# Layer 0 and self-attention of 32 images: another first image, another running minimum, another last convolution

## The chip, the cores and the metric

The kernel runs on one core of a Trainium2 chip. Its time is the device time of one execution in microseconds. The core has five engines with a queue each: TensorE (PE in the profile; PEld are its weight loads), VectorE (DVE), ScalarE (ACT), GpSimd (POOL) and SyncE (SP, which here only issues DMAs). They run independently and wait for one another through semaphores. Matmuls write into PSUM[...]; all else lives in SBUF.

## The reference

The input x has shape (32, 64, 56, 56): 32 images of 64 channels and N = 3136 pixels. All is float32.

```python
# layer 0: within each of 8 groups of 8 channels, all products of two and of three channels
x = x + (conv2(products of 2) + b2) * beta2 + 0.1 * (conv3(products of 3) + b3) * beta3
# layer 1, for each image, l is the result of layer 0
g = clip(batchnorm(w_inside @ l), 0, 6)        # (64, N)
theta = l[:32]                                 # (32, N)
f = theta.T @ theta                            # (N, N)
f = softmax(softmax(f, axis=1), axis=2)        # once over the rows, once over the columns
out = g @ f.T / 56 * 56
out = batchnorm(depthwise_conv3x3(out)) + l
```

f is symmetric, so a softmax over its first axis and one over its second can be made from the same rows of scores.

## The kernel before

**Pairs and tiles.** Images are worked on in 16 pairs A and B. The N rows of an image's scores are cut into tiles of 128; the tiles of a pair are 24 of A, one for the tails of both, and 24 of B: IT = 49, and 784 in all. `scores` (L477 on) makes a tile in two halves of 1568 columns: four matmuls theta^T theta of 392 columns into the four banks of a PSUM tile `ps` (of which there is one), then one eviction on DVE, `e<-ps`. It copies the half into an SBUF tile `e` (of which there are four), times 1.0, and its accumulator writes the maximum of each row into `mx`. After both halves `first_softmax` reduces the two maxima on DVE to `nm`, the negated maximum, and ACT makes Exp(e + nm) with the sum of each row; for the tile before, `second_softmax` takes the reciprocal of that sum on DVE and ACT makes the second Exp. LAG = 3 tiles later `attend` multiplies the tile with g on PE into `av` and `ax` (banks of PSUM). A pair's result is divided on DVE, turned and brought by DMA into `tt`.

**Layer 0.** `products` multiplies channels with shifted channels: for a chunk of columns (PCS: 13 chunks of 242, the last 232) and two groups of 32 slots. `load_next` loads x with the channels shifted over the partitions (tiles `x`, `xa`, `xb`), and the centre channels (`xc`), which takes two DMAs whose source is two groups of 32 rows. The products are multiplied with the weights on PE (`poly`), and `poly_out` adds a bias and the centre channels on DVE and writes `y`, the layer's result. For all images but the first the products are made on POOL, and matmuls and outputs are spread over the tiles of the pair before; the second image's work lies in the tiles of the first. For the first image there is nothing to spread it over: its products are made on DVE, its loads are issued by SP and ACT by turns, and `first_poly` writes its sums into PSUM banks of their own (`pp`, `pq`). The row groups of g are made behind the chunks (`first_g`). Then `load_theta` copies theta from `y` to the four partition groups by four DMAs, and the first tile's scores can begin.

**The convolution.** The depthwise convolution of pair n is 45 steps on DVE: NB = 5 blocks of rows times 9 taps, each a SCALAR_TENSOR_TENSOR (`y` = `tt` shifted times a weight, plus `y`); `conv_begin` adds the bias on POOL first, `store` writes a finished block to `out`. The steps are spread over the gaps of the next pair's tiles. The last pair has no next pair: its 45 steps follow its last tile back to back.

**What sets the order.** Every engine's order is written out: `Pinned` makes each instruction follow the one issued before it on the same engine, and its helper `call` is line L109, the line of every instruction in the profile. The loop over tiles issues work by slots ("loads", "feed", "gap0", "gap1", "aux0") that `put` fills by tile number; `feed` and `advance` issue loads and products as their buffers come free and as a budget (`credit`) allows. At most eight DMAs are under way at a time: they go through eight semaphores in turn.

Of the kernel before, what the change touches and what calls it, by code (L numbers as in the profile page):

```python
# [9 lines left out]
FP = mybir.dt.float32  # L10
AF = mybir.ActivationFunctionType
ALU = mybir.AluOpType
AX = mybir.AxisListType
# [20 lines left out]
NK = 3  # L34
# [36 lines left out]
def tile_poly_conv_attention(  # L71
# [123 lines left out]

    b3row = const.tile([128, C], FP, name="b3row")
# [13 lines left out]
    dve.tensor_tensor(bias0, bias0, t0, ALU.add)  # L210

# [9 lines left out]
    for k in range(GM):  # L221
# [13 lines left out]
    yt = yp.tile([128, 3, N], FP, name="y")  # L235
    ys = [yt[:, p, :] for p in range(3)]
    pool.memset(ys[0][C:, :], 0.0)
    prods = {}
    NB = 5
    BLK = [(b * H // NB, (b + 1) * H // NB) for b in range(NB)]  # L240
    stored = set()

    LOADS = {
        "0": [(0, 1, 0, 0)],
        "a": [(0, 1, 0, 1)],
        "2": [(0, 1, 2, 0)],
        "4": [(0, 1, 4, 0)],
        "b": [(0, 2, 5, 0), (1, 2, 1, 0)],  # L250
    }
# [11 lines left out]
    def start(out, in_, queue=sync):  # L263
        credit[0] -= 1
        queue.dma_start(out=out, in_=in_)

    def load_next():
        tag, key = plan.pop(0)
        n, c, ks, name, k, queue = key
        p0, w = PCS[c]  # L270
        held[tag] += 1
        ident = f"{n}_{c}_{ks[0]}_{k}"
        if name == "c":
            t = xp.tile([128, 2, PCH], FP, name=f"xc_{ident}", tag=tag, bufs=XB[tag])
            at = slice(ks[0] * 32, ks[-1] * 32 + 32)
            for d in range(2):
                src = bass.AP(
                    x.tensor,
                    ((4 * n + ks[0]) * EXT + 4 * d) * 4 * N + p0,
                    [[EXT * 4 * N, len(ks)], [N, 32], [1, w]],  # L280
                )
                start(t[at, d, :w], src, queue)
            loaded[key[:-1]] = [t[at, d, :w] for d in range(2)]
            return
        t = xp.tile([128, PCH], FP, name=f"x{name}_{ident}", tag=tag, bufs=XB[tag])
        for s0, every, d, grow in LOADS[name]:
            src = bass.AP(
                x.tensor,
                ((4 * n + k) * EXT + d) * 4 * N + p0,
                [[N, 32], [grow * 4 * N, NSLOT // every], [1, w]],  # L290
            )
            start(t[s0::every, :w] if every > 1 else t[:, :w], src, queue)
        loaded[key[:-1]] = t[:, :w]
# [9 lines left out]
    def products(n, c, ks, eng):  # L303
# [16 lines left out]
        for k in ks:  # L320
            yield "load", (n, c, ks, "a", k)
            x0[k] = use("0", k)
            xa = use("a", k)
            q = prp.tile([128, PCH], FP, name=f"q_{ident}_{k}", tag="q", bufs=ROOM["q"])[:, :w]
            eng.tensor_tensor(q, x0[k], xa, ALU.mult)
            rounds[0][k] = q
            held["xs"] -= 1
            prefetch()
        for r, of in enumerate(("0", "2", "4", "b")):
            rounds.append({})  # L330
            yield "pr", len(ks)
            for k in ks:
# [4 lines left out]
                eng.tensor_tensor(p, rounds[0][k], xr, ALU.mult)  # L337
# [8 lines left out]
        eng.tensor_tensor(p4, both[0], both[1], ALU.mult)  # L346
# [27 lines left out]
    def feed(n, c, ks, eng):  # L374
# [3 lines left out]
        for tag, name, k in todo:  # L378

            queue = act if eng is dve and len(plan) % 2 else sync  # L380
            plan.append((tag, (n, c, ks, name, k, queue)))
        feeds.append((products(n, c, ks, eng), None))
# [12 lines left out]
    def poly(n, c, ks, rs, acc=None):  # L395

# [3 lines left out]
        own = acc is not None  # L402
        if not own:
            acc = ax[:, AUX:]
        at = slice(ks[0] * 32, ks[-1] * 32 + 32)
        for r in rs:
            for k in ks:
                pe.matmul(
                    out=acc[k * 32 : k * 32 + 32, :w],
                    lhsT=wq[:, r, k % 2, :] if r < NRND else w4[at, k * 32 : k * 32 + 32],  # L410
                    rhs=rounds[r][k],
                    start=own and r == 0,
# [5 lines left out]
    def poly_out(n, c, ks, acc=None):  # L418

        if acc is None:  # L420
            acc = ax[:, AUX:]
# [6 lines left out]
            ys[n % 3][at, p0 : p0 + w], acc[at, :w], bias0[at], xc, ALU.add, ALU.add  # L428
# [5 lines left out]
    def load_theta(b):  # L434
        y = ys[b // 2 % 3]
        p0 = (b % 2) * C
        th = thp.tile([128, N], FP, name=f"th_{b}", tag=f"th{b % 2}")
        for r in range(4):
            start(th[r * 32 : r * 32 + 32, :], y[p0 : p0 + CRED, :])
        ths[b] = th  # L440
# [36 lines left out]
    def scores(t, half):  # L477
        n, kind, q = tile_at(t)
        if half == 0:
            es[t] = ep.tile([128, N], FP, name=f"e_{t}", tag="e")  # L480
            mx = sp.tile([128, 2], FP, name=f"mx_{t}", tag="mx")
            nm = sp.tile([128, 1], FP, name=f"nm_{t}", tag="nm")
            z = sp.tile([128, 1], FP, name=f"z_{t}", tag="z")
            rz = sp.tile([128, 1], FP, name=f"rz_{t}", tag="rz")
            stats[t] = mx, nm, z, rz
        p = ps.tile([128, HALF, BANK], FP, name=f"ps_{t}_{half}", tag="ps")
        for j in range(HALF):
# [12 lines left out]
        e = es[t][:, half * HALF * CH : (half + 1) * HALF * CH]  # L500
        dve.tensor_scalar(
            e.rearrange("p (j c) -> p j c", c=CH), p[:, :, :CH], 1.0, None, ALU.mult, ALU.max,
            accum_out=stats[t][0][:, half : half + 1],
        )

    def first_softmax(t):
        mx, nm, z, _ = stats[t]
        dve.tensor_reduce(nm, mx, AX.X, ALU.max, negate=True)
        act.activation(es[t], es[t], AF.Exp, bias=nm, scale=1.0, accum_out=z)

    def second_softmax(t):
        _, _, z, rz = stats.pop(t)
# [82 lines left out]
    def conv_begin(n, b):  # L595
        blk = ys[n % 3][:, BLK[b][0] * W : BLK[b][1] * W]
        pool.tensor_scalar(blk, blk, bias2, None, ALU.add)

    def conv_step(n, i):
        b, i = divmod(i, 9)  # L600
        k, dy, dx = TAPS[i]
        r0, r1 = max(BLK[b][0], 1 - dy), min(BLK[b][1], H + 1 - dy)
        x0, x1 = max(0, 1 - dx), min(W, W + 1 - dx)
# [10 lines left out]

    def store(n, b):
        stored.add((n, b))
        blk = slice(BLK[b][0] * W, BLK[b][1] * W)
# [73 lines left out]
    put(-1, "aux0", lambda: [feed(0, c, ONE, dve) for c in range(NPC)])  # L691
    put(-1, "aux0", lambda: prepare(FOR_G))
    banks = {}

    def bank(c):
        k, r = divmod(c, HALF + NK)
        if r == 0:
            t = ps.tile([128, HALF, BANK], FP, name=f"pp_{k}", tag="ps")
            banks.update({k * (HALF + NK) + i: t[:, i, :] for i in range(HALF)})
        if r >= HALF:  # L700
            banks[c] = pa.tile([128, BANK], FP, name=f"pq_{c}", tag=f"av{r - HALF}")
        return banks[c]

    def first_poly(c):
        acc = bank(c)
        for r in range(NRND + 1):
            advance()
            poly(0, c, ONE, [r], acc)
        advance()
        poly_out(0, c, ONE, acc)  # L710

    def first_g(c):
        for qs in GS:
            if ready(qs) == c:
# [4 lines left out]
    for c in range(NPC):  # L719
        put(-1, "aux0", lambda c=c: first_poly(c))  # L720
        if c:
            put(-1, "aux0", lambda c=c: first_g(c - 1))
    put(-1, "aux0", lambda: load_theta(0))
    put(-1, "aux0", lambda: first_g(NPC - 1))

# [5 lines left out]
    for n in range(NP):  # L731
# [50 lines left out]
        if n == 0:  # L782
            put(0, "feed", lambda: [feed(0, c, TWO, pool) for c in range(NPC)])
        if n + 1 < NP:
            put(
                max(base - 8, 1), "feed",
                lambda n=n: [feed(n + 1, c, ALL, pool) for c in range(NPC)],
# [10 lines left out]
    for n in range(NP):  # L798
        t0 = n * IT + IT + LAG + 5
        more = range(2 * t0, 2 * ((n + 2) * IT - 1))  # L800
        if n + 1 < NP:
            more = [h for h in more if h // 2 != (n + 1) * IT + NQ + LAG]
            more = [h for h in more if h not in leaves] if len(more) - len(leaves & set(more)) >= 9 * NB else more
        for i in range(9 * NB):
            at = more[i * (len(more) - 1) // (9 * NB - 1)] if n + 1 < NP else 2 * t0 + i
# [10 lines left out]
    run(-1, "aux0")  # L816
# [119 lines left out]
```

## Time and profile before

| what | value |
| --- | --- |
| time, median of 3 runs | 5033.5 us (5032.83 to 5038.3) |
| the profiled execution's own time | 5033.6 us |
| its span in the profile | 5031.8 us |
| granted TensorE clock, mean over the span | 0.983 |
| first eviction starts at | 146.92 us |
| one pair in the middle (first eviction to the next pair's first) | 295.15 us |
| the first pair | 404 us |
| the last pair's convolution starts at | 4988.90 us |

The span is the time from the first recorded instruction to the last. A row of the timeline reads: start, duration in us, engine, line, operation, output<-inputs by tile name, shapes, and how many instructions are merged in it; in brackets the idle time of the engine just before and what ended it. A row of the groups has the busy sum and the mean of one in ns, then the idle time before and its releaser. A row of the stretches gives busy time (and number of instructions) of each engine between two times, then the granted TensorE clock as a share of full speed, the mean busy share of the 16 DMA engines and the bandwidth. A float32 matmul appears as two records.

### The profile page before, as it was taken

Reading aid. Unit: us, or ns where it says so; the run is one execution under the profiler, and the core shown is the slowest. Engines: PE = TensorE matmul, PEld = TensorE weight load, DVE = VectorE, ACT = ScalarE, POOL = GpSimd, SP = SyncE. Lnnn points to the kernel's source line nnn. Section 1 sums busy time; section 2 is a strip of 40 time slices with the busy share of each in tenths; the row PEclk is TensorE's granted clock in tenths of the full one; section 3 lists DMA queues with packets and bytes.
Section 4 is the critical chain, followed back from the end, with each engine's and each line's share of the span. In section 5 each row is a group of like instructions: output and inputs, shape, how many; then the busy total and the mean of one; then the engine's idle time right before and its main releaser. Section 6 shows DMA issues by size and latency. Waiting matters only on the chain.

```text
span 5031.8 us, 240733 instructions
## 1 busy us (share of the span) xinstructions
PE 4753.8 (94%) x105924; PEld 3340.6 (66%) x105924; DVE 4222.6 (84%) x6962; ACT 4545.5 (90%) x2356; POOL 3194.2 (63%) x4325
## 2 busy tenths in 40 slices
PE   3898999999999999999999999999999999999995
PEld 1465676776767677676766767676676767667663
DVE  4465698898989889898988989898898989889887
ACT  0577899999999999999999999999999999999995
POOL 0667585876858587585857758586775858677000
PEclk7899999999999999999999999999999999999998
DMA  5555656555565555655565565556556555654201
GB/s 144 140 153 152 150 147 149 145 146 143 143 147 144 147 142 144 145 147 139 152 149 137 142 148 148 139 149 149 143 137 145 151 142 145 151 139 120 44 10 33
DMA packets 892956, 684.17 MB, mean 136 GB/s; under 512 B 291584, under 2 KB 877568, under 8 KB 887808
## 3 DMA queue, kind: packets, MB, share of 16 engines
q1 hardware_dynamic: 879368, 659.52, 51.4%
q8 instruction: 828, 13.57, 1.1%
q10 hardware_dynamic: 12536, 9.25, 0.7%
q14 instruction: 224, 1.84, 0.1%
HBM read 565.65 MB, written 25.69 MB: 118 GB/s over the span
## 4 chain that ended last, share of the span: by engine, by line
PE 71%; DVE 21%; DMA 4%; issue 2%; POOL 1%; SPq 1%; ACT 0%; ACTq 0%; POOLq 0%; DVEq 0%
PE av L109 30%; PE ps L109 24%; PE ax L109 16%; DVE e L109 15%; DVE y L109 3%; DMA xc_None<-in_x_dram 2%; DVE num L109 1%; DMA xa<-in_x_dram 1%; SPq L109 1%; POOL p L109 1%; DMA x<-in_x_dram 1%; DVE rd L109 0%; DVE nm L109 0%; POOL q L109 0%; DMA xb<-in_x_dram 0%
## 5 line engine op out<-in xcount | busy, mean ns | idle before, releaser
L109 DVE TENSOR_SCALAR_CACHE_REDUCE e<-ps 128x1568 f32<-128x1568 f32 x1568 | 2806.6, 1790 | 508.1 <-PE ps L109 462.9
L109 PEld LDWEIGHTS av<-gq,e 128*64 128x64 f32 x64512 | 2014.1, 138 | 864.7 <-issue 806.7
L109 ACT ACTIVATE e<-e,nm 128x3136 f32<-128x3136 f32 x784 | 2282.8, 2912 | 310.8 <-DVE rz L109 228.3
L109 POOL TENSOR_TENSOR p<-q,x 128x242 f32<-128x242 f32 (+1 forms) x2418 | 1781.1, 769 | 939.6 <-PE ax L109 843.0
L109 ACT ACTIVATE e<-e,rz 128x3136 f32<-128x3136 f32 x784 | 2270.3, 2896 | 0.0
L109 PE MATMUL av<-gq,e 128*64 128x65 f32 x64512 | 2227.2, 225 | 3.9 <-ACT e L109 3.2
L109 PE MATMUL ps<-th 32*128 32x392 f32 (+1 forms) x12800 | 1489.4, 541 | 109.7 <-DVE e L109 96.7
L109 PEld LDWEIGHTS ps<-th 32*128 32x128 f32 (+1 forms) x12800 | 491.3, 181 | 448.0 <-DVE e L109 368.4
L109 DVE SCALAR_TENSOR_TENSOR y<-tt,wdt,y 128x605 f32<-128x605 f32 (+4 forms) x720 | 742.4, 1032 | 6.7 <-DMA tt<-tr 5.3
L109 POOL TENSOR_TENSOR p<-q,xb 128x242 f32<-128x242 f32 x806 | 592.5, 762 | 230.6 <-PE ax L109 218.1
L109 POOL TENSOR_TENSOR q<-x,xa 128x242 f32<-128x242 f32 x806 | 561.5, 722 | 216.0 <-DMA xa<-in_x_dram 208.2
L109 PE MATMUL ax<-gq,e 128*64 128x65 f32 x12288 | 489.7, 222 | 0.0
L109 PE MATMUL ax<-p,wq 128*32 128x242 f32 (+1 forms) x6448 | 481.5, 373 | 1.5
L109 PEld LDWEIGHTS ax<-gq,e 128*64 128x64 f32 x12288 | 425.3, 138 | 0.0
L109 POOL TENSOR_SCALAR y<-y,bias 128x616 f32<-128x616 f32 (+1 forms) x80 | 162.8, 2036 | 147.5 <-PE ax L109 137.7
L109 PEld LDWEIGHTS ax<-p,wq 128*32 128x32 f32 x6448 | 178.9, 109 | 111.4 <-POOL p L109 18.8
L109 DVE SCALAR_TENSOR_TENSOR y<-ax,bias,xc_None 128x242 f32<-128x242 f32 (+3 forms) x208 | 97.1, 467 | 108.8 <-PE ax L109 103.1
L109 POOL TENSOR_TENSOR p<-xc_None 128x242 f32<-128x242 f32 (+3 forms) x208 | 127.6, 614 | 78.8 <-DMA xc_None<-in_x_dram 68.6
L109 PE MATMUL ax<-wit,y 128*64 128x64 f32 x3136 | 143.8, 223 | 18.6 <-DVE ax L109 9.6
L109 PE MATMUL ax<-p,w 128*32 128x242 f32 (+1 forms) x1612 | 123.9, 369 | 31.6 <-POOL p L109 31.6
L109 ACT ACTIVATION_READ_ACCUMULATOR e<-e,nm 128x1 f32 x784 | 145.6, 186 | 0.0
L109 DVE TENSOR_REDUCE nm<-mx 128x1 f32<-128x2 f32 x784 | 121.7, 155 | 27.2
(73 smaller groups left out, 1368.1 us busy)
## 6 DMA issues: line engine op xcount, KB each, us to landing
x<-in_x_dram SPq DMA_DIRECT2D x2268, 121.0 KB
xb<-in_x_dram SPq DMA_DIRECT2D x1512, 60.5 KB
xa<-in_x_dram SPq DMA_DIRECT2D x756, 121.0 KB
th<-y SPq DMA_DIRECT2D x128, 392.0 KB
xc_None<-in_x_dram SPq DMA_DIRECT2D x360, 121.0 KB
x<-in_x_dram SPq DMA_DIRECT2D x190, 116.0 KB
out_dram<-y SPq DMA_DIRECT2D x64, 308.0 KB
tt<-tr SPq DMA_DIRECT2D x128, 100.0 KB
```

The costliest lines, as they stand in the source:

```text
L109: i = f(*args, **kw)
```

## The change

1. **The first image** is worked in 7 chunks of 448 columns (FCS), by functions of its own. `first_loads` issues 16 DMAs per chunk, by SP and ACT in turn, into a ring of 28 slots in the four `e` tiles; the centre channels are loaded in four DMAs of 32 rows. `first_products` makes 11 products on DVE into 21 slots that lie in `y`'s two later parts and in `tt`. `first_poly`, `first_out` and `first_g` follow one chunk apart. Theta is copied in two parts, the first five chunks and the rest, and the second image's first twelve loads are issued between the two.
2. **The running minimum.** The eviction multiplies by −1 and accumulates the minimum; the second half starts from the first half's minimum, read from `nm`. The TENSOR_REDUCE is gone; the first Exp takes scale −1 and the minimum as its bias.
3. **The last pair's convolution** has 7 blocks of 8 rows. Blocks 0 to 3 are steps on DVE as before; blocks 4 to 6 are 27 matmuls of `tt` with diagonal matrices of the tap weights (`make_diags`, on POOL early in the last pair) into one PSUM tile, and a DVE operation per block merges them with the bias and `y`.

The diff, cut to its core (the parameters `queue` and `eng` of `feed`, `products` and `start` and the accumulator parameter of `poly` fall away, since only POOL's products are left there):

```diff
+    FW = N // 7
+    FCS = [(p, FW) for p in range(0, N, FW)]
+    firsts = [ep.tile([128, N], FP, name=f"first_{i}", tag="e") for i in range(4)]
...
+    fx, fp = parts(firsts), parts(ys[1:] + [tt])
...
+    def first_loads(c):
+        p0, w = FCS[c]
+
+        def load(dst, k, d, grow, steps):
+            src = bass.AP(x.tensor, (k * EXT + d) * 4 * N + p0, [[N, 32], [grow * 4 * N, steps], [1, w]])
+            if steps == 1:
+                src = bass.AP(x.tensor, (k * EXT + d) * 4 * N + p0, [[N, 32], [1, w]])
+            (act if fat["q"] % 2 else sync).dma_start(out=dst, in_=src)
+            fat["q"] += 1
+
+        for name, k in [(a, k) for k in (0, 1) for a in "0a"] + [(a, k) for a in "24b" for k in (0, 1)]:
...
+            for s0, every, d, grow in LOADS[name]:
+                load(t[s0::every, :] if every > 1 else t, k, d, grow, NSLOT // every)
+        for d in (0, 1):
...
+            for k in (0, 1):
+                load(t[k * 32 : k * 32 + 32, :], k, 4 * d, 0, 1)
+
+    def first_products(c):
...
+        q = {k: product(xs["0", k], xs["a", k]) for k in (0, 1)}
+        frs[c] = [q] + [{k: product(q[k], xs[a, k]) for k in (0, 1)} for a in "024b"]
+        dve.tensor_tensor(xs["c", 1], xs["c", 0], xs["c", 1], ALU.mult)
+
+    first_loads(0)
+    first_loads(1)
+    first_products(0)
...
+    first_products(1)
+    first_loads(2)
...
-    BLK = [(b * H // NB, (b + 1) * H // NB) for b in range(NB)]
+    BLK = [[(b * H // NB, (b + 1) * H // NB) for b in range(NB)]] * (NP - 1)
+    BLK.append([(r, r + 8) for r in range(0, H, 8)])
+    NDVE = 4
...
-    def load_theta(b):
+    def load_theta(b, c0=0, c1=N):
...
-            start(th[r * 32 : r * 32 + 32, :], y[p0 : p0 + CRED, :])
+            start(ths[b][r * 32 : r * 32 + 32, c0:c1], y[p0 : p0 + CRED, c0:c1])
...
         dve.tensor_scalar(
             e.rearrange("p (j c) -> p j c", c=CH),
-            p[:, :, :CH], 1.0, None, ALU.mult, ALU.max,
-            accum_out=stats[t][0][:, half : half + 1],
+            p[:, :, :CH], -1.0, nm[:, :1] if half else None, ALU.mult, ALU.min,
+            accum_out=nm[:, half : half + 1],
         )
...
     def first_softmax(t):
-        mx, nm, z, _ = stats[t]
-        dve.tensor_reduce(nm, mx, AX.X, ALU.max, negate=True)
-        act.activation(es[t], es[t], AF.Exp, bias=nm, scale=1.0, accum_out=z)
+        nm, z, _ = stats[t]
+        act.activation(es[t], es[t], AF.Exp, bias=nm[:, 1:], scale=-1.0, accum_out=z)
...
+    def make_diags():
+        eye = xp.tile([128, PCH], FP, name="eye", tag="xs", bufs=XB["xs"])[:, :128]
+        pool.memset(eye, 0.0)
+        pool.affine_select(out=eye, in_=eye, ...)
+        for k in range(9):
...
+            pool.tensor_scalar(t, eye, wdt[:, k : k + 1], None, ALU.mult)
+
+    def conv_matmuls(n, blocks):
+        acc = ps.tile([128, HALF, BANK], FP, name="conv", tag="ps")
+        for j, b in enumerate(blocks):
+            for i in range(9):
...
+                pe.matmul(
+                    out=o[:, r0 - rb : r1 - rb, x0:x1],
+                    lhsT=diags[k],
+                    rhs=tr[:, r0 + dy - 1 : r1 + dy - 1, x0 + dx - 1 : x1 + dx - 1],
...
+    def conv_end(n):
+        blocks = range(NDVE, len(BLK[n]))
+        accs = conv_matmuls(n, blocks)
+        done = 0
+        for b in range(NDVE):
+            for i in range(9):
+                conv_step(n, 9 * b + i)
+            store(n, b)
+            while done < len(blocks) and (b + 1) * len(blocks) >= (done + 1) * NDVE:
+                m = blocks[done]
+                y = ys[n % 3][:, BLK[n][m][0] * W : BLK[n][m][1] * W]
+                dve.scalar_tensor_tensor(y, accs[m], bias2, y, ALU.add, ALU.add)
+                store(n, m)
+                done += 1
...
+    fb = ps.tile([128, HALF, BANK], FP, name="first_s", tag="ps")
+    banks = [fb[:, i, :] for i in range(HALF)]
+    banks += [pa.tile([128, BANK], FP, name=f"first_{i}", tag=f"av{i}") for i in range(NK)]
...
+    first_poly(0)
+    for c in range(1, NF):
+        first_poly(c)
+        first_out(c - 1)
+        if c + 2 < NF:
+            first_loads(c + 2)
+        if c + 1 < NF:
+            first_products(c + 1)
+        if c == 5:
+            load_theta(0, 0, FCS[5][0])
+            for b in range(NPC):
+                feed(0, b, TWO)
+            credit[0] = 12
+            advance()
+        first_g(c - 1)
+    first_out(NF - 1)
+    load_theta(0, FCS[5][0], N)
+    first_g(NF - 1)
...
+        if n + 1 == NP:
+            put(n * IT + LAG + 1, "feed", make_diags)
...
+            put(t0, "gap0", lambda n=n: conv_end(n))
```

## The prediction

> **What bounds the kernel now.** I read the engine totals first, then the chain that ended last, then busy time by stretch.
>
> ```profile
> span 5031.8 us, 240733 instructions
> PE 4753.8 (94%) x105924; PEld 3340.6 (66%) x105924; DVE 4222.6 (84%) x6962; ACT 4545.5 (90%) x2356; POOL 3194.2 (63%) x4325
> ...
> core 0: us, PE busy (x) PEld busy (x) DVE busy (x) ACT busy (x) POOL busy (x), PEclk, DMA share, GB/s
> 100.00:120.00 20.00, 9.73 (x60) 4.01 (x60) 10.01 (x28) 0.00 (x0) 0.00 (x0) 0.61 0.61 166
> ...
> 160.00:460.00 300.00, 273.41 (x5138) 171.99 (x5130) 169.04 (x299) 211.50 (x111) 223.04 (x337) 0.98 0.57 150
> 2260.00:2560.00 300.00, 294.84 (x6733) 209.69 (x6730) 265.58 (x434) 288.67 (x151) 209.11 (x282) 1.00 0.56 144
> ...
> 4970.00:5032.00 62.00, 7.68 (x256) 7.40 (x252) 43.42 (x57) 6.97 (x4) 0.00 (x0) 0.61 0.17 43
> ```
>
> Four stages with four limits. In the middle (2260 to 2560) PE is busy 295 of 300 us: TensorE is the bound, ACT 11 us behind. The first pair is looser (273 and 212). In the head (100 to 120) no engine is busy more than half, and at the end only DVE works. The change touches the head (part 1), every tile (part 2) and the end (part 3), so each is costed in its own stage.
>
> The head, in the timeline, and the DMA row of 105 to 115 in slices of 0.25 us:
>
> ```profile
> 105.26 0.45 DVE L109 SCALAR_TENSOR_TENSOR y<-pp,bias,xc_None 64x242 f32<-64x242 f32 x1
> ...
> 112.17 0.40 DVE L109 TENSOR_TENSOR p<-xc_None 64x242 f32<-64x242 f32 x1 [2.33 <-DMA xc_None<-in_x_dram]
> ...
> 113.90 0.46 DVE L109 SCALAR_TENSOR_TENSOR y<-pp,bias,xc_None 64x242 f32<-64x242 f32 x1
> ...
> 135.24 4.73 SPq L109 DMA_DIRECT2D th<-y  x4
> ...
> 146.92 1.79 DVE L109 TENSOR_SCALAR_CACHE_REDUCE e<-ps 128x1568 f32<-128x1568 f32 x1 [8.42 <-PE ps L109]
> ...
> DMA  7573177369775669899986685116511103757612
> ```
>
> One chunk of 242 columns takes 113.90 − 105.26 = 8.64 us, and DVE waits in it for the centre rows (xc). The last output of layer 0 comes near 135.2, then four copies of theta (392 KB each), and the first eviction starts at 146.92.
>
> **Part 1, the head.** The same 3136 columns come in 7 chunks of 448. A loop whose cycle is set by data per column gains nothing from that by itself, so what sets the 8.64 us matters. The DMA share is 0.61: by the mean, 0.61 × 8.64 = 5.3 us of engine time per chunk. But the DMA row shows slices of 1 and 0 between fuller ones: at one tenth, two of sixteen engines work. The Trainium skill, "DMA: Bandwidth & Descriptors", section "Why a DMA increments its semaphore by 16 and not by 1" (how many engines), says that a transfer is spread over the largest number up to 16 that divides the slowest dimension of both its patterns. The xc load's source has a slowest dimension of 2 (two row groups): two engines. The changed loads take 32 rows with slowest dimension 32: sixteen. In the trace a packet of 968 bytes takes 56 ns on average. Per chunk every engine has 80 packets of the other loads (4.5 us), and by the rule the two have 128 ÷ 2 = 64 more: 144 × 56 ns = 8.1 us against 8.64 measured. By the mean share alone the loads would not be the limit and rearranging them would gain little; I follow the rule, because it gives the measured cycle and the low slices.
>
> After: 88 packets per engine and chunk of 1792 bytes. The trace has 69 ns for 1536 bytes and 101 for 2464, so about 78: 6.9 us. DVE per chunk: ten products on 128 rows at 0.335 us each (six take 2.01 us at 242 columns) plus 206 more columns[...]: 5.5 us; the centre product 0.55, the output 0.6, and the pairs of copies for g (0.34 and 0.36, 9 or so over 7 chunks) 0.9: 7.6 us. The order of the changed program adds a wait: the output of chunk c stands behind the matmuls of chunk c+1, because the first four chunks share one PSUM tile, so DVE idles 0.5 to 1 us in three chunks. So about 8.3 us per chunk in the middle, 7.5 at the end.
>
> ```profile
> 20.68 2.01 DVE L109 TENSOR_TENSOR p<-q,x 128x242 f32<-128x242 f32 x6
> ```
>
> Chunk 0's products run to 20.5, constants to 22.2, chunk 1's to 28.5, batch-norm constants to 34.1, then outputs at 34.8, 42.7, 50.8, 58.3, 65.9, 73.4 and 76.4 (no more products). The second part of theta (columns 2240 on, 115 KB per copy) is issued 76.6 to 79 and lands at 81; the first part went at 66, under the products. First eviction near 82: 146.9 − 82 = **−65**. Bounds: DVE at its bare 7.6 gives −72; loads that queue on the eight outstanding transfers allowed, at 10.5 us per chunk, give −50.
>
> Also moved: twelve loads of the second image now stand on SP's queue ahead of theta's second part (about 0.6 us an issue, 7 us from 66 on, done by 74). They lead the first eviction by some 13 us instead of 7. The first pair takes 404 us against 295.15 later and waits for xc loads and POOL; I give it **−5** (−9 to 0).
>
> **Part 2, the evictions.** It removes this row, and turns the second half's eviction from two constants into one that reads its start value from SBUF:
>
> ```profile
> L109 DVE TENSOR_SCALAR_CACHE_REDUCE e<-ps 128x1568 f32<-128x1568 f32 x1568 | 2806.6, 1790 | 508.1 <-PE ps L109 462.9
> ...
> L109 DVE TENSOR_REDUCE nm<-mx 128x1 f32<-128x2 f32 x784 | 121.7, 155 | 27.2
> ...
> 18.28 0.23 DVE L109 TENSOR_SCALAR wdt<-wdt,r_bn 128x9 f32<-128x9 f32 x1
> ...
> 4931.93 1.79 DVE L109 TENSOR_SCALAR_CACHE_REDUCE e<-ps 128x1568 f32<-128x1568 f32 x1 [0.25 <-PE ps L109]
> 4933.79 0.94 PE L109 MATMUL ps<-th 32*128 32x392 f32 x8 [0.26 <-DVE e L109]
> ```
>
> 121.7 us of DVE go, but the middle is bound by PE, so not from the time. What PE feels of DVE is the lower pair: it waits for an eviction's end to reuse the PSUM tile. Eviction, hand-over both ways and scores matmuls make 1.01 + 1.79 + 0.06 = 2.86 us per half, a floor of 5.72 per tile. A middle tile takes 5.72 to 6.02; slack by half is 0.14 after second halves and 0.05 after first ones, often none. A longer eviction therefore costs PE directly. Rows for the price of a pointer: a TENSOR_SCALAR with one on 9 columns takes 0.233 us, its like with constants 0.150 (+0.08); three-operand forms against plain ones are +0.05. I take +0.065 on 1.79. In the middle: the 49 second halves of a pair lose about 0.65 us where slack is short, and the freed reduce, which lay ahead of late first halves, gives 0.43 back; +0.2 × 14 pairs = 3. The last pair runs on the floor: 48 × 0.065 = 3. The first pair waits for data elsewhere, 0. Together **+6**; bounds −9 (no pointer cost, only the reduce's gain) and +9 (0.08).
>
> **Part 3, the end.**
>
> ```profile
> 4988.90 39.59 DVE L109 SCALAR_TENSOR_TENSOR y<-tt,wdt,y 128x616 f32<-128x616 f32 x45 [5.32 <-DMA tt<-tr]
> 4996.77 32.11 SPq L109 DMA_DIRECT2D out_dram<-y  x5
> ...
> 9.06 2.04 PE L109 MATMUL ax<-wq,w 128*128 128x256 f32 x4 [9.06 <-DMA w<-in_wpoly_dram]
> ...
> 129.79 1.80 PE L109 MATMUL pq<-p,wq 128*32 128x242 f32 x16
> ```
>
> 45 steps take 39.59 us, 0.88 each: [...]0.24 is fixed. A step of 448 columns takes 0.47 + 0.24 = 0.71. DVE keeps 36 steps (25.6) and gets three merges (2.1): 27.7, that is −12. But the three blocks sit in one PSUM tile, and in the changed program the first merge waits for the last of 27 matmuls, and behind that merge in DVE's order stand the two other merges, 18 steps and five of the seven stores. Their price: the row at 129.79 holds eight matmuls of 242 columns (two records each), two of them side by side in different columns of the array: 1.80 ÷ 4 = 0.45 us per pair, 1.86 ns a column. So 448 columns take 0.83 us, 27 of them 22.5, at a full clock. The row at 9.06 is cold: two full-array matmuls of 256 columns in 2.04, 4 ns a column, hence 27 × 448 × 4 = 48 us. The Trainium skill, "TensorE: Matmul & The Clock Gate", Part 1, says TensorE drops to half clock after an idle window of 3.4 us and returns after a busy one; here the granted clock is 0.50 from 4983 on, while the last copies of the attention are awaited. By the full clock alone 22.5; with half-clock matmuls for the first window or so +3: 25.5; if PE stayed cold, 48. I take 25.5 (24 to 28), since the middle shows 1.00 under load. Then DVE does 18 steps in 12.8, idles until 25.5, and still has three merges and 18 steps (14.9): 40.4 against 39.6, **+1**, where the edit's purpose alone would give −12. Eleven small POOL operations for the diagonal matrices lie beside the last pair, which has no products to make for a next pair; without that cover they would be some 11 × 0.77 = 8 us (0.77 is POOL's mean for a product). Two stores more at 0.6 us of issue lie behind DVE's steps; the last one is smaller (448 columns for 616).
>
> **Sum.** The profiled execution took 5033.6 us (span 5031.8), 0.1 above the median of 5033.5. 5033.6 − 65 − 5 + 6 + 1 = 4970.6: **4970 us**.
>
> **Rivals.** *The head is bound by loads still* (15%): eight outstanding transfers, 0.6 us an issue on two queues and landings that grew to 12 us before speak for it; then 10.5 us per chunk, −50: 4985. *PE stays cold at the end* (7%): the low clock there speaks for it, 27 dense matmuls against; +21: 4991. *The pointer is free and the clock returns at once* (12%): −9 instead of +6, tail −2: 4952. *The long eviction decides against the change* (5%): past the 0.14 us of slack every excess counts in 784 tiles, and 0.09 × 784 = 70 us eat what the head gains. So from 0.23 us for the pointer (a second half of 2.02 us) the kernel is slower than before; at 0.25 it takes 5033.6 − 69 + 0.11 × 784 = 5051. Against it, no row shows a pointer above 0.08. *The head gains nothing* (1%, 5035): that the loads or their order cost 16 us per chunk, twice DVE's own 7.6.
>
> **Numbers.** The main case has 60%, with 4958 to 4982 as its own range. The range, 4950 to 4993, takes in the three neighbours and leaves out the slow eviction, the head without gain and the ends of the others. 10 us (0.2%) is what a measurement can tell from no change: faster 0.94, same 0.02, slower 0.04.
>
> **To look for.** First eviction near 82 (75 to 97), y outputs 7.5 to 8.3 us apart; no long waits for centre rows in the head; second-half evictions near 1.85 us, first halves 1.79; middle pairs 295 to 296 us; the first merge 25 us after the last conv starts, with DVE idle for 12 us before it, PE clock back at 1. Wrong if chunks take over 10 us, if an eviction passes 2 us, or if the first merge comes at 13 or at 48 us.

## The result and the profile after

The changed kernel takes 4996.2 us (median of four runs, 4985.5 to 5001.3) against 5034.9 for the kernel before, timed beside it: a ratio of 0.992 (95% interval 0.9901 to 0.9939), 39 us less. The forecast was 4970 with a range to 4993, so the direction held and the size did not. The four runs lie 16 us apart, where the four of the kernel before lie within 5.5; the profiled execution is one of the long ones (5000.1 us).

The first lines of its page, then busy time by stretch (columns as before):

```profile
span 4998.3 us, 239445 instructions
PE 4773.4 (95%) x105834; PEld 3345.3 (67%) x105834; DVE 4135.0 (83%) x6100; ACT 4552.7 (91%) x2356; POOL 3205.0 (64%) x4335
...
40.00:60.00 20.00, 17.11 (x91) 6.42 (x92) 18.39 (x40) 0.00 (x0) 0.00 (x0) 0.87 0.86 264
160.00:460.00 300.00, 273.24 (x5261) 174.29 (x5256) 164.70 (x260) 209.58 (x109) 220.47 (x332) 0.97 0.57 148
2260.00:2560.00 300.00, 294.11 (x6713) 209.08 (x6708) 260.03 (x380) 289.04 (x151) 207.46 (x278) 1.00 0.57 144
```

The head has become another stage: VectorE busy 18.4 of 20 us and DMA at 0.86, where they had 10.0 of 20 and 0.61. The middle is as it was. Cut at the first eviction of each pair, the two profiled executions compare like this:

| stretch | before, us | after, us | difference | forecast |
| --- | --- | --- | --- | --- |
| start to first eviction | 146.9 | 90.6 | −56.3 | −65 |
| first pair | 404.0 | 407.0 | +3.1 | −5 |
| pairs 1 to 14, without the two long steps below | 4134.3 | 4134.9 | +0.6 | +3 |
| what two long convolution steps add to two of these pairs | 0 | 16.3 | +16.3 | 0 |
| last pair, to its convolution | 303.7 | 307.3 | +3.6 | +3 |
| last convolution to the end | 42.9 | 42.1 | −0.8 | +1 |
| span | 5031.8 | 4998.3 | −33.5 | −63 |

The long steps are in the timeline of VectorE, and beside it GpSimd's for the same stretch (start, duration, engine, line, operation):

```profile
3895.51 7.38 DVE L108 SCALAR_TENSOR_TENSOR y<-tt,wdt,y 128x616 f32<-128x616 f32 x1
3902.81 1.78 DVE L108 TENSOR_SCALAR_CACHE_REDUCE e<-ps 128x1568 f32<-128x1568 f32 x1
...
3894.94 2.69 POOL L108 TENSOR_TENSOR q<-x,xa 128x242 f32<-128x242 f32 x4
3897.59 4.64 POOL L108 TENSOR_TENSOR p<-q,x 128x242 f32<-128x242 f32 x7
...
3904.66 1.69 PE L108 MATMUL ps<-th 32*128 32x392 f32 x8 [6.06 <-DVE e L108]
```

The same step of the same pair in the kernel before, and GpSimd's operations beside it:

```profile
3948.80 0.87 DVE L109 SCALAR_TENSOR_TENSOR y<-tt,wdt,y 128x616 f32<-128x616 f32 x1
...
3947.65 3.25 POOL L109 TENSOR_TENSOR q<-x,xa 128x242 f32<-128x242 f32 x4
```

One convolution step of 616 columns, 0.84 to 1.45 us in other pairs, takes 7.38. GpSimd runs eleven operations in a row beside it, without a pause, until 3902.23; the step ends 0.66 us later, and the next eviction, on which TensorE waits, has to stand behind it. The same step of the next pair takes 7.40. These two pairs last 303.4 us, most others 295.2: each loses 8.2, more than the some 6 us that the step itself is longer. TensorE stood idle for 6.06 us, its granted clock was 0.50 from 3902.2 to 3909.0, and its first scores after the pause took 1.69 us instead of the usual 0.94.

The head's SP queue, which shows when the moved loads and theta's second part really went:

```profile
73.75 3.63 SPq L108 DMA_DIRECT2D first<-in_x_dram  x6
77.48 4.00 SPq L108 DMA_DIRECT2D th<-y  x4
81.52 1.36 SPq L108 DMA_DIRECT2D x<-in_x_dram  x1
...
88.24 2.53 SPq L108 DMA_DIRECT2D xb<-in_x_dram  x4
90.87 2.48 SPq L108 DMA_DIRECT2D th<-y  x4
```

SP is busy with the first image's loads up to 77.4. Only then come theta's first part, the second image's twelve loads, and at 90.87 theta's second part, though its data had been ready near 86.6. The first tile's second half waits for it: 9.8 us for the tile instead of 7.2.

The two forms of the eviction in the groups, and the end:

```profile
L108 DVE TENSOR_SCALAR_CACHE_REDUCE e<-ps 128x1568 f32<-128x1568 f32 x784 | 1403.6, 1790 | 328.1 <-PE ps L108 300.4
L108 DVE TENSOR_SCALAR_CACHE_REDUCE e<-ps,nm 128x1568 f32<-128x1568 f32 x784 | 1448.3, 1847 | 254.7 <-PE ps L108 251.3
...
4956.22 12.54 DVE L108 SCALAR_TENSOR_TENSOR y<-tt,wdt,y 128x448 f32<-128x448 f32 x18 [5.20 <-DMA tt<-tr]
4980.77 0.68 DVE L108 SCALAR_TENSOR_TENSOR y<-conv,bias,y 128x448 f32<-128x448 f32 x1 [12.01 <-PE conv L108]
...
4957.74 22.99 PE L108 MATMUL conv<-tt,diag 128*128 128x448 f32 x54 [10.02 <-DMA tt<-tr]
```

The pointer costs 1847 − 1790 = 57 ns. VectorE stands 12.01 us before the first merge, until the last of the 27 matmuls.

### The profile page after: what moved, and what is told of

The parts are those of the page before. It is cut to its first block, busy times and chain, and to the rows that moved or that the text cites. A ratio compares the mean times of both kernels' runs of the same rounds, so it can differ in the third digit from the quotient of the medians.

```text
span 4998.3 us, 239445 instructions
## 1 busy us (share of the span) xinstructions
PE 4773.4 (95%) x105834; PEld 3345.3 (67%) x105834; DVE 4135.0 (83%) x6100; ACT 4552.7 (91%) x2356; POOL 3205.0 (64%) x4335
## 4 chain that ended last, share of the span: by engine, by line
PE 78%; DVE 12%; DMA 3%; ACT 2%; POOL 1%; issue 1%; SPq 1%; ACTq 0%; DVEq 0%; POOLq 0%
PE av L108 34%; PE ps L108 26%; PE ax L108 18%; DVE e L108 10%; ACT e L108 2%; SPq L108 1%; DMA xc_None<-in_x_dram 1%; POOL p L108 1%; DVE y L108 1%; DMA x<-in_x_dram 1%; DVE num L108 1%; PE first_s L108 0%; PE conv L108 0%; DMA xa<-in_x_dram 0%; DMA first<-in_x_dram 0%
## 5 line engine op out<-in xcount | busy, mean ns | idle before, releaser
L108 POOL TENSOR_TENSOR p<-q,x 128x242 f32<-128x242 f32 (+1 forms) x2418 | 1816.3, 784 | 953.1 <-PE ax L108 945.0
L108 DVE TENSOR_SCALAR_CACHE_REDUCE e<-ps 128x1568 f32<-128x1568 f32 x784 | 1403.6, 1790 | 328.1 <-PE ps L108 300.4
L108 DVE TENSOR_SCALAR_CACHE_REDUCE e<-ps,nm 128x1568 f32<-128x1568 f32 x784 | 1448.3, 1847 | 254.7 <-PE ps L108 251.3
L108 DVE SCALAR_TENSOR_TENSOR y<-tt,wdt,y 128x605 f32<-128x605 f32 (+6 forms) x711 | 723.6, 1018 | 6.3 <-DMA tt<-tr 5.2
L108 POOL TENSOR_TENSOR p<-q,xb 128x242 f32<-128x242 f32 x806 | 570.8, 735 | 227.8 <-PE ax L108 220.8
L108 POOL TENSOR_SCALAR y<-y,bias 128x616 f32<-128x616 f32 (+2 forms) x79 | 145.9, 1847 | 98.6 <-PE ax L108 98.6
```

Of the source, the lines that this page charges most:

```text
L108: i = f(*args, **kw)
```

## The experiments

The start of the first eviction is the mark of the head's end. The kernels of experiments 1 and 5 to 8 were timed once, with the profile, so they are compared by stages; their totals count only together, in experiment 2.

**1. The centre rows' DMA engines, both ways round.** In the changed kernel, one DMA of 64 rows in two groups where it has two of 32; in the kernel before, four of 32 rows where it has two of 64.

```diff
-            for k in (0, 1):
-                load(t[k * 32 : k * 32 + 32, :], k, 4 * d, 0, 1)
+            src = bass.AP(x.tensor, 4 * d * 4 * N + p0, [[EXT * 4 * N, 2], [N, 32], [1, w]])
+            (act if fat["q"] % 2 else sync).dma_start(out=t[:C, :], in_=src)
```

> The changed kernel with the centre rows of the first image loaded in one DMA of 64 rows per operand (source in two groups of 32 rows) where it has two DMAs of 32. Theory (such a load runs on two of the sixteen DMA engines): per chunk these two have 80 packets of the other loads and 64 more, 144 of about 92 ns = 13 us a chunk where the others have 7.4, so outputs of layer 0 come 11 to 13 us apart from the third chunk on and the first eviction near 115 (105 to 122) instead of 90.6. Rival (the mean DMA share is what counts, the number of engines of one load does not): two issues fewer per chunk and nothing else, first eviction 88 to 91.

> The kernel before, with the first image's centre rows loaded by 32 rows in four DMAs per chunk where it has two of 64 rows in two groups. Nothing else differs: 13 chunks, old eviction, old convolution. Theory (two engines set the 8.64 us of a chunk): 86 packets of 56 ns = 4.8 us on every engine, DVE's own 4.3 to 5 us and 16 issues by two queues at 0.6 us = 5 us are then alike, so chunks come 5.5 us apart (5 to 6.5), first eviction near 146.9 - 12 x 3.1 = 109 (103 to 120), total about 5033 - 38 = 4996. Rival (the chunk's size and loop order made the gain of the change): first eviction 143 to 148, total 5033.

Measured: the changed kernel's first eviction went from 90.6 to 109.8, with outputs 13.1, 12.3 and 11.6 us apart and waits like this one before the centre product:

```profile
76.63 0.67 DVE L108 SCALAR_TENSOR_TENSOR y<-first_s,bias,first 64x448 f32<-64x448 f32 x1
...
87.75 0.62 DVE L108 TENSOR_TENSOR first<-first 64x448 f32<-64x448 f32 x1 [3.04 <-DMA first<-in_x_dram]
88.95 0.67 DVE L108 SCALAR_TENSOR_TENSOR y<-first,bias,first 64x448 f32<-64x448 f32 x1
```

The rule by the slowest dimension holds here, and by the number: 13 us were worked out from 144 packets. The other way round the gain was much less than I had put down: the kernel before with loads by 32 rows has chunks 7.4 to 8.3 us apart (8.5 to 9.7 before the edit; the last three, with no products behind them, are shorter in both), not 5.5, its first eviction at 135.2 (−11.7) and 5021.0 us in one run against 5032.7. Between 60 and 112 us VectorE's waits for centre rows fell from 9.2 us to 4.7 and those for xb from 10.7 to none, but it now waits 11.1 us for x and xa, where it had waited 0.4:

```profile
91.97 0.40 DVE L109 TENSOR_TENSOR p<-xc_None 64x242 f32<-64x242 f32 x1 [1.45 <-DMA xc_None<-in_x_dram]
93.22 0.41 DVE L109 TENSOR_TENSOR q<-x,xa 128x242 f32<-128x242 f32 x1 [0.85 <-DMA xa<-in_x_dram]
```

So of the head's 56 us, the two-engine loads account for 12 to 19 (measured from either side). The remaining 37 to 45 are what is left for the wider chunks with their own loads and buffers (16 DMAs per chunk then carry 448 columns, where 14 carried 242); no run took these apart.

**2. Part 2 undone, and part 2 alone.** The old eviction and reduce in the changed kernel; the turned scores, running minimum and no reduce in the kernel before. The edits are those of the diff.

> The changed kernel with the old eviction (constants, maximum) and its TENSOR_REDUCE put back: part 2 undone. Theory 1 (the long convolution step of 7.4 us on VectorE in two pairs of the profile is a lost fight for a shared port of SBUF with GpSimd, decided by the moment at which the step starts; without the reduce the step starts 0.1 us later in GpSimd's operation): with the reduce back the steps start as before, no step over 1.5 us, runs within 4 us of one another, near 4985.5 - 3 (last pair's pointer cost) = 4980 to 4985. Rival (the stalls come with the new head, whose work shifts the loads of later pairs): runs spread by steps of 8 us as those of the changed kernel (4985 to 5001), and long steps in the trace.

> The kernel before with part 2 alone (turned scores, running minimum, no reduce). Theory 1 (stalls by the moment at which a convolution step starts): second-half evictions 1.847 us, last pair 3 us longer, middle pairs as before or up to 0.2 us longer, so 5036 to 5039 in a run without a stall, and runs with one, two or more stalls 8 us apart: a spread of 8 to 24 us, with steps over 5 us in some profiles. Rival (stalls come with the new head): all runs within 4 us, 5035 to 5040. Rival (the freed 0.155 us per tile counts in the middle): about 5033 - 5 or less.

Measured: without part 2 the changed kernel takes 4976.4 us (4969.4 to 4978.8), below the 4980 that I had put as the least, and its profile has no long step. That is 56 us less than the kernel before beside it (5032.7), where the changed kernel had been 39 less. Part 2 alone takes the kernel before from 5032.7 to 5049.5: its nine runs spread from 5032.4 to 5055.2, while fourteen of the kernel before lie between 5029.5 and 5036.5. The nine are not cleanly 8 us apart (5032, 5033, 5038, 5041, 5050, 5052, 5052, 5053, 5055), and the one with a profile is the shortest and has no long step, so what its other runs lost was not seen.

What part 2 does to the step can be read from the traces. In the nine profiles that have part 2 and this step in its old place, it starts 0.52 to 0.56 us after the end of GpSimd's last finished operation, in each of thirteen pairs. Of these 117 starts 99 took about 1.4 us, 13 took 0.84 and 5 took 7.4. In the five profiles with the old eviction, 63 of 65 starts come at 0.40 to 0.46 and none took over 1.02. The kernel before with part 2 alone is one of the nine: its thirteen starts stand at 0.53 to 0.56, though none was lost in that run. So part 2 moves the step by 0.1 us into a place where it can be lost.

The totals agree. Seven kernels of experiments 1 and 5 to 8 keep part 2 and the step's place. With their differences in the first eviction taken off, and for one each that in the first pair and at the end, the five without a long step took 4977 to 4984 us, the one with one 4993 and the one with two 5000. The changed kernel's profiled run, with two, took 5000.1.

The new head is not needed for the spread, and part 2 is not its only source. Beside experiments 3 and 9, 5 of 28 runs of the kernel before took 5040 to 5046 us, and the first kernel of experiment 9, with the old eviction, has a long step elsewhere.

**3. The step moved by hand.** The step that lasted 7.4 us goes to the next half tile's gap.

```diff
-            at = more[i * (len(more) - 1) // (9 * NB - 1)]
+            at = more[i * (len(more) - 1) // (9 * NB - 1) + (i == 20)]
```

> The changed kernel with one convolution step of each pair (the third of its third block, the one that lasted 7.4 us in two pairs) moved to the gap of the next half tile; all else as in the changed kernel, part 2 included. Theory (that step starts 0.12 us before the end of a GpSimd operation and then sometimes loses the shared port of SBUF for GpSimd's whole run of 11 operations): runs within 6 us of one another, near 4984 (4980 to 4988), no step over 2 us. Rival (part 2 costs its 20 us in another way, the long steps are only where it shows): still 4985 to 5001, spread by steps of 8 us.

Measured: worse, 5033.0 us, from 5016.7 to 5052.6. I had taken any other place to be safe. In the new one the step lasts 4.55 to 4.60 us in 8 of 14 pairs, in which GpSimd has 6 operations in a row instead of 11 (in the first row below the step and a short one behind it are merged):

```profile
1242.64 5.43 DVE L108 SCALAR_TENSOR_TENSOR y<-tt,wdt,y 128x616 f32<-128x616 f32 x2
...
1241.85 4.68 POOL L108 TENSOR_TENSOR p<-q,x 128x242 f32<-128x242 f32 x7
```

GpSimd's run ends at 1246.53, the step alone (4.55 us) at 1247.19, again 0.66 later. A shorter run gives a shorter stall with the same end: that is the direct evidence for the mechanism, from an experiment that failed at what it was meant for. The pairs without a long step also take 1 us more than in the changed kernel (296.2 to 296.4 us, most of them), which I can't explain.

**4. A dummy reduce.** The changed kernel with a TENSOR_REDUCE back in the old place, its result unused; pointer and minimum stay.

```diff
+        idle = sp.tile([128, 1], FP, name=f"idle_{t}", tag="idle")
+        dve.tensor_reduce(idle, nm, AX.X, ALU.min)
         act.activation(es[t], es[t], AF.Exp, bias=nm[:, 1:], scale=-1.0, accum_out=z)
```

> The changed kernel with a TENSOR_REDUCE of 0.155 us put back where the old one stood, its result used by nobody: pointer and turned scores stay, only VectorE's timing of the gaps goes back to about what it was. Theory (part 2 costs by the long convolution steps, which come from the moment at which a step starts against GpSimd's operations): no step over 2 us, runs within 8 us of one another, 4981 to 4988. Rival (the long steps come with the pointer eviction, whatever the phase): 4985 to 5001 as the changed kernel, or above.

Measured: 4989.7 us, 4987.3 to 4993.2, no long step in the profile. The four runs lie 6 us apart; that the median is 6 us below the changed kernel's is not clear of noise (ratios of 0.991 and 0.992 with overlapping intervals). The step did not go back to its old moment either: it mostly starts 0.48 to 0.62 us after GpSimd's last operation, not 0.40 to 0.46. The level is above what I expected: the middle pairs take 295.8 to 296.2 us. It is tempting to read from this that the pointer costs a middle pair 0.6 to 1.0 us and that the freed reduce gives as much back, but experiment 3 has pairs of 296.2 us without any reduce, so this is not shown.

**5. Theta ahead of the early loads.** The feed of the second image and its twelve loads are moved behind theta's second part.

> The changed kernel with theta's second part issued before the second image's first twelve loads. Theory (the twelve loads delay theta's second part on SP's queue by 4.3 us, and the first tile waits for it): second eviction 3.5 to 4.5 us after the first where the changed kernel has 6.15, first eviction unchanged near 90 or up to 2 us earlier, first pair 402 to 407. Rival (the early loads of the second image earn what they cost): first pair longer by as much as the first tile is shorter, 409 or more. Single total: not compared, the long steps of part 2 spread it by 16 us.

Measured: the second eviction follows the first by 3.69 us instead of 6.15, at 93.41. But the first pair takes 407.0 (407.0 before the edit): what the first tile gains is lost again by the third, and from there the second image is waited for. The theory is right on the tile, the rival on the pair.

**6. The square roots ahead, twice.** First all of the batch-norm constants moved between the first and the second chunk's loads; then only their additions and roots.

```diff
     first_loads(0)
+    for v, s in roots.values():
+        act.activation(s, v, AF.Sqrt)
     first_loads(1)
```

> The changed kernel with the batch-norm constants made between the first and second chunk's loads (and so before the first products) where it has them behind the second chunk's products. Theory (the wait of 4.6 us for ACT's square root, which stands behind ACT's load issues, and the constants' 5 us of DVE work delay the first output): first output of layer 0 at 33 to 36 instead of 41.0, first eviction at 83 to 87 instead of 90.6, less than the 6 us because chunks then wait for loads. Rival (the loads set the pace of the head at 9 us a chunk): outputs of the last chunks and the first eviction unchanged within 1.5 us.

> The changed kernel with only the two additions and square roots of the batch-norm constants made ahead, the roots on ACT between its issues for the first and second chunk; the rest of the constants stays where it is. Theory (the wait of 4.6 us for the square root behind ACT's issues delays the first output and with it the head): no wait at the constants, first output at 36.5 to 38.5 instead of 41.0, first eviction 86 to 88.5. Rival (the loads set the head's pace): the outputs of the fifth to seventh chunk and the first eviction (87.5 to 90.8 in the runs so far) unchanged, with more waits of VectorE for loads in chunks 3 to 6.

Measured, in the changed kernel first (ACT's issues, its load of a table, and VectorE's wait for the root):

```profile
19.46 14.73 ACTq L108 DMA_DIRECT2D first<-in_x_dram  x16
34.23 1.28 ACT L108 ACT_TABLE_LOAD   x1 [34.23 <-DMA first<-in_x_dram]
...
35.81 0.55 DVE L108 RECIPROCAL r_bn<-s_bn 128x64 f32<-128x64 f32 x1 [4.61 <-ACT s_bn L108]
```

The first form has its first output at 45.1, later than the 41.0 of the changed kernel, because the second chunk's loads on ACT now stand behind both roots; the first eviction is at 90.8. That form mixes two things, but an output 4 us later that costs nothing at the head's end means that slack was there: its later chunks hardly wait for loads. The second form has no wait at the constants, the first output at 37.7 and the first eviction at 86.4, as the theory said. Eight profiles with the head unchanged have it at 87.5 to 90.6, and the second form has it at 85.1 in experiment 9, so the wait is worth some 3 to 4 us of the head. Chunk 5 still waits 3 us for loads.

**7. Three PSUM tiles for the last blocks.**

```diff
-        acc = ps.tile([128, HALF, BANK], FP, name="conv", tag="ps")
+        accs = [pa.tile([128, BANK], FP, name=f"conv_{j}", tag=f"av{j}") for j in range(len(blocks))]
```

> The changed kernel with the last convolution's three matmul blocks in three PSUM tiles of their own (those of the attention's sums, free by then) where it has one tile. Theory (the first merge waits for all 27 matmuls because they share a tile): no wait before the first merge, VectorE's 39 operations back to back, last convolution 27 to 28 us from first step to last merge instead of 39.0, last eviction to end of span 12 us shorter. Rival (TensorE's half clock makes even the first block late): first merge waits 3 us or more, 30 us or more.

Measured, in VectorE's timeline of that kernel:

```profile
4935.35 12.54 DVE L108 SCALAR_TENSOR_TENSOR y<-tt,wdt,y 128x448 f32<-128x448 f32 x18 [5.22 <-DMA tt<-tr]
4947.81 0.68 DVE L108 SCALAR_TENSOR_TENSOR y<-conv,bias,y 128x448 f32<-128x448 f32 x1
4948.40 6.39 DVE L108 SCALAR_TENSOR_TENSOR y<-tt,wdt,y 128x448 f32<-128x448 f32 x9
```

No wait is left; from the first step to the end of the span it takes 30.0 us instead of 42.1. The 12 us that the division of the work offers were held back by the shared tile, not by TensorE's clock, which starts as low here: the matmuls take 23.0 us as before.

**8. What paces the first pair.** The second image's centre rows by 32 rows: first in four DMAs per chunk (16 DMAs per chunk in all), then in two with both operands each (14, as before).

```diff
+            if ks == TWO:
+                for i in ks:
+                    src = bass.AP(x.tensor, (4 * n + i) * EXT * 4 * N + p0, [[N, 32], [16 * N, 2], [1, w]])
+                    start(t[i * 32 : i * 32 + 32, :, :w], src)
```

> The changed kernel with the second image's centre rows, too, loaded by 32 rows in four DMAs per chunk where it has two of 64. Theory (the first pair is paced by the second image's chunks, 9.3 us each, and a part of that is the wait of GpSimd for centre rows from two DMA engines): chunks 8.3 to 8.8 us apart (GpSimd's own 11 operations of 0.75 us are 8.3), the second image done some 8 to 13 us earlier, first pair 394 to 400 us instead of 403 to 407. Rival (eight transfers under way at a time and SP's issues set the 9.3 us): first pair 403 or more.

> The changed kernel with the second image's centre rows in two DMAs per chunk as before, but each of 32 rows with both operands (so on sixteen engines) where each had 64 rows of one operand. Theory (SP's issues, 14 a chunk of 0.646 us, pace the first pair, since 16 a chunk took it from 9.3 to 10.4 us): chunks 9.0 to 9.4 us apart and the first pair 401 to 408 us. Rival (waits for centre rows from two engines pace it): chunks 8.3 to 8.8 us, first pair 394 to 400.

Measured: with four, the first pair takes 422.6 us, 16 more; GpSimd's products of centre rows come 10.7 us apart over thirteen chunks instead of 9.6. With two, 406.3, and 9.7 us apart; the thirteenth chunk's output comes 123.2 us after the first eviction against 126.5, within what the other profiles differ by (119.2 to 126.7). SP's issues follow one another by 0.646 us (median): 14 make 9.0 of the 9.6 us and 16 make 10.3 of the 10.7. So the second image's chunks are paced by the number of DMAs, whatever their engines. Whether it is SP's issues or the eight transfers under way that count, these runs can't tell, and fewer than 14 were not tried.

**9. Put together.** First the old eviction, three PSUM tiles and four-DMA centre rows; then the old eviction, three tiles and early roots.

> The changed kernel with the old eviction and reduce, the last convolution's matmul blocks in three PSUM tiles, and the second image's centre rows by 32 rows. Theory: 4976.4 (old eviction) - 12 (three tiles) - 5 to 9 (first pair) = 4955 to 4960, runs within 6 us of one another, no convolution step over 2 us before the last pair. If the first pair is paced by issues: 4963 to 4966.

> The changed kernel with the old eviction and reduce, the last convolution's matmul blocks in three PSUM tiles, and the square roots made ahead; the second image's loads as in the changed kernel. 4976.4 (old eviction) - 12.1 (three tiles) - 2 (first pair ends 1 to 3 us earlier with the roots ahead) = 4962 (4956 to 4968), and no convolution step over 2 us if the phase against GpSimd is that of the kernel with the old eviction. If the roots' gain is eaten in the first pair: 4964 to 4966.

Measured: the first 4990.8 us (4980.7 to 4994.9). It has the four DMAs of experiment 8 and carries their loss (first pair 419.6), and another step, in the next pair, lasts 5.46 us. The second takes **4962.7 us** (4960.7 to 4969.1), as worked out, a ratio of 0.9862 (0.9845 to 0.9878) to the kernel before, with no long step in its profile. It is better than both kernels: it leaves out part 2 and mends parts 1 and 3.

## Why the prediction was wrong

The span came down by 33.5 us in the profiled run where 63 were forecast. Of the 29.5 between them, the long steps are 16.3, the head 8.7 and the first pair 8.1; the other terms give 3.6 back.

- **Part 2, the freed reduce.** The step that failed. The prediction's terms for the eviction held or were too dear (the pointer 57 ns for 65, the last pair +3.6 for +3, the middle +0.6 for +3). But it counted the 121.7 us of the reduce as time that is hidden or gives 0.43 us a pair back, and took every other duration on VectorE as fixed. With the reduce gone and the eviction longer, the convolution step starts 0.1 us later against GpSimd's operations (experiment 2), and in two pairs it then waited for GpSimd's whole run: +16.3 us, where the prediction had nothing. Without these the profiled execution would stand at 5000.1 − 16.3 = 4983.8, inside the range. How many steps a run loses is luck (none, one or two in the profiles of kernels with part 2): of the changed kernel's four runs two lie inside the range and two outside. The text named GpSimd only for its own small additions.
- **Part 1, what set the old cycle.** The two-engine loads did, but only just: with them mended alone the old chunk still took about 7.8 us, not 5 to 6 (experiment 1). That the head's term came out near (−56 for −65) rests on the 448 columns and on the sum for the new chunk, which was right: a product of 448 columns took 0.54 us for 0.55, and the first outputs came 7.9, 7.9 and 7.7 us apart for 8.3 to 7.5.
- **Part 1, the head's start.** "Batch-norm constants to 34.1": they ended near 40.9. The first chunks' products ended 2.5 us late, behind their loads, and then VectorE waited 4.6 us for the root on ACT. I had the root there and did not count that ACT first issues the third chunk's half of the loads (3.0 us of the wait) and loads a table (1.28).
- **Part 1, packets of 1792 bytes at "about 78" ns.** They took 91 on average in the trace. So DMA had 8.0 us of work per chunk, as much as VectorE, and chunk 5 waited 3.3 us for loads: its output came 10.9 us after the fourth's, past the 10 us that was named as a sign of being wrong.
- **"Twelve loads ... done by 74".** SP was held by the first image's loads until 77.4, so they went from 81.5 to 90.8 and delayed theta's second part. I had counted the moved step's own issues and put them on an empty queue.
- **The first pair, −5.** I named xc loads and GpSimd; it is the 14 DMAs per chunk (experiment 8), which the change does not touch. The second image's first output comes 15.3 us after the first eviction where it came 12.8 before, so the loads lead by less, not by more; and theta's delay adds nothing (experiment 5).
- **Part 3 was right.** The first merge came 24.6 us after the first step for 25.5, after a wait of 12.0; the end changed by −0.8 for +1. A step took 0.70 us for 0.71. The half clock cost the first four matmuls 3 us, as put down: the granted clock was 0.50 when they began and 1.00 from 6.0 us later on. It came back under load, as the Trainium skill's "TensorE: Matmul & The Clock Gate", Part 1, has it, but later than one busy window of 3.4 us. Only the price at full clock was too high. At full clock the 27 matmuls follow one another by 0.74 us (20 in all for 22.5): the row at 129.79, divided by four, had counted the last pair's own run in.
- **A sum.** The rival "the pointer is free" adds up to 4954, not 4952.

The rival nearest to the outcome in its number is "the head is bound by loads still" (4985), and for the head alone it was partly so. None of the rivals had the long steps.

## What to carry to other kernels

An edit that shortens one engine's gap work also shifts when that engine's two-input SBUF operations meet GpSimd's. Look for operations on VectorE that last as long as a run of GpSimd's, and count a change of that moment as a term of its own. A stall of TensorE costs more than its length if the clock drops meanwhile (here 8.2 us for some 6). Where a consumer waits for part of a PSUM tile that several matmuls fill, count to the last matmul into the tile, not into the part. When DMAs are moved, write down the queue's own timeline first: what is ahead of them, at the measured spacing of issues, decides when they go.

## What the runs showed of the hardware

The Trainium skill, "SBUF — State Buffer", section "SBUF: two separate sides", says that a VectorE operation with two SBUF inputs and a GpSimd operation that reads SBUF exclude one another, and that whichever starts first holds the shared port for the whole instruction. The ordinary steps agree: a step that takes 0.84 us alone and about 1.4 beside GpSimd has waited out most of one GpSimd operation of 0.7 us. The long ones go beyond it: VectorE waited not for one instruction but for a whole unbroken run of 6 or 11, so GpSimd's next operation got in ahead of the waiting step each time.

Over the profiles of all sixteen kernels there are 14 steps over 2 us. Thirteen of them end 0.655 to 0.661 us after GpSimd's run; the fourteenth, in the first combination of experiment 9, ends inside it and is not explained. The eight of experiment 3 are one step of one kernel and began 0.036 to 0.056 us after GpSimd's operation before the one under way had ended; the other five are one step of three kernels and began 0.517 to 0.539 us after. Some 490 steps that began in these two windows took less than 1.5 us. So the moment goes with the loss but does not fix it, and what decides inside the window stays open. I did not expect a stall of nine times the step's length.
